# Quantized down projection: subtracting from the rows in two VectorE steps, normalisation placed behind the next tile's steps

## The chip, the core and the metric

The kernel runs on one core of a Trainium2 chip. The core has TensorE (matrix products, PE in the profile), VectorE (DVE), ScalarE (ACT), GpSimd (POOL) and SyncE (SP, here the issuer of most transfers), each with its own queue of instructions that it works through in order, and semaphores between them. The metric is the device time of one execution in microseconds; the figure shown is the median of several runs. One further execution is profiled, and its trace is what the text reads.

## What is computed

Two transformer layers on rows `x` of 2 batches x 512 rows x 512 columns, with a normalisation after every half layer. The change lies in the second half of layer 0, a feed-forward with ternary weights and truncation to 8-bit integers, and in what follows it, the attention of layer 1:

```python
x = layernorm(x + L0_attn(x))          # linear attention with a memory
# L0_ffn, quantized
xf = x / 128.0
gate = einsum("bsh,ih->bsi", xf, w_gate)
up = einsum("bsh,ih->bsi", xf, w_up)
inter = silu(gate) * up
inter_q = trunc(clip(inter * 128.0, -128.0, 127.0)).astype(int8)
down = einsum("bsi,hi->bsh", inter_q.astype(float32), w_down)
out = trunc(clip(down * 128.0, -128.0, 127.0)).astype(int8)
x = layernorm(x + out)
x = layernorm(x + L1_attn(x))          # softmax attention, one head of 128
x = layernorm(x + L1_ffn(x))           # silu(x Wg) * (x Wu), then Wd
```

`layernorm` takes the mean from each row of 512 and divides by the root of the variance plus 1e-5. The inner width of both feed-forwards is 1376, cut into 11 blocks (ten of 128 and one of 96).

## The kernel before

**Rows and order.** The 1024 rows are eight tiles of 128 rows x 512 columns, `xs[b][t]`, numbered i = 0 to 7 by `order`: tiles 0 to 3 are batch 0, tiles 4 to 7 batch 1. They stay on the core from layer to layer and are changed in place.

**Who sets the order.** All engines but GpSimd get their order of instructions from a scheduler, which starts from the order of the program and may put an instruction ahead of another that is not ready by its reckoning. GpSimd's order is that of the program as written (line 59). `tc.issue_after(ins)` keeps what is issued under it, on the engine of `ins`, behind `ins`. Each engine then follows its list strictly.

**Up half of the feed-forward (`up(b, c)`, lines 515 to 553).** For a batch and one of the 11 blocks TensorE makes gate (`pg`) and up (`pu`) in 16 matmuls, ScalarE takes the Silu (`sg`), VectorE the product (`y`, line 538) and cuts it to 12 leading bits (line 152), ScalarE makes two integer parts of it (lines 162 and 163), and VectorE joins them into `it` (line 545). The two parts are `ta`, an int8 of the positive part, and `tb`, an int16 of the negative part; the truncated value is `min(tb, 128) - ta` up to the sign that the scale carries.

**Down half (lines 570 to 614).** `down(b, t)` makes one tile of 128 rows in 11 matmuls into `pd`. `f0_down(i)` is one step of a hand-written pipeline over the eight tiles:

- `scaled(i)`: ScalarE scales `pd` into `yd` (line 592), VectorE cuts it (line 152);
- `added(i - 1)`: ScalarE makes `ta` and `tb` (lines 162, 163), VectorE joins them into `w` (line 600), GpSimd subtracts `w` from the rows (line 601);
- for tile i - 2, the statistics: VectorE `bn_stats` and `bn_aggr` (lines 132, 134), then GpSimd adds epsilon and takes the power -0.5 (lines 140, 141) into `rstd`;
- for tile i - 3, the normalisation of the rows on VectorE (line 146).

So a tile that goes through in one step of the loop has its normalisation three steps later. The calls (lines 646 to 655) run the up half's last blocks, three steps, the very last block `up(1, 10)`, four steps, then the transposes of batch 0 for the attention (`transposed(xs[0], "a10")`), then the rest.

**What follows.** `transposed` (lines 105 to 127) turns the four normalised tiles of a batch on TensorE (line 113), 16 transposes of 128 x 128 into four PSUM tiles, each of which needs all four row tiles; ScalarE copies two of them out (line 124) and VectorE the other two (line 126). From the copies TensorE makes queries and keys (`pqk`, line 752) and values (`pv`, line 765), then the same for batch 1 from tiles 4 to 7. Meanwhile GpSimd adds an output bias to all row tiles (line 805), ScalarE and VectorE split the first weights of the last feed-forward into parts (lines 675 to 689), and SyncE loads weights for it into the buffers that the quantized feed-forward has left. Then come the scores (line 779), and from about 308 us on the last feed-forward's products (lines 912 and 987).

Of the kernel before, what the change touches and what calls it, by code (L numbers as in the profile page):

```python
# [10 lines left out]
F32 = mybir.dt.float32  # L11
# [4 lines left out]
ALU = mybir.AluOpType  # L16
# [3 lines left out]
P = 128  # L20
B, S, HID = 2, 512, 512
# [15 lines left out]
def kernel(  # L37
# [19 lines left out]
    nc = tc.nc  # L57
# [14 lines left out]
    xs = [[], []]  # L72
# [32 lines left out]
    def transposed(rows, name, by_tile=False):  # L105

        xt = xtp.tile([P, NK, S], F32, tag="xt", name=f"xt_{name}")
        pts = {}

        def turn(k, t):  # L110
            if k not in pts:
                pts[k] = psum(f"pt_{name}_{k}")
            nc.tensor.transpose(pts[k][:, ts(t, P)], rows[t][:, ts(k, P)], ident)

        if by_tile:
            for t in range(NT):
                for k in range(NK):
                    turn(k, t)
        for k in range(NK):
            if not by_tile:  # L120
                for t in range(NT):
                    turn(k, t)
            if k % 2 == 0:
                copies.append(nc.scalar.copy(xt[:, k, :], pts[k]))  # L124
            else:
                copies.append(nc.vector.tensor_copy(xt[:, k, :], pts[k]))
        return xt

    def layernorm_stats(row, name):

        st = small.tile([P, 6], F32, tag="st", name=f"st_{name}")
        nc.vector.bn_stats(st, row)
        mv = small.tile([P, 2], F32, tag="mv", name=f"mv_{name}", bufs=8)
        nc.vector.bn_aggr(mv, st)
        return root(mv, name)

    def root(mv, name):

        rstd = small.tile([P, 1], F32, tag="rstd", name=f"rstd_{name}", bufs=8)
        nc.gpsimd.tensor_tensor(rstd, mv[:, 1:2], ln_eps, ALU.add)  # L140
        nc.gpsimd.tensor_tensor(rstd, rstd, minus_half, ALU.pow)
        return mv, rstd

    def layernorm_apply(out, row, stats):
        mv, rstd = stats
        nc.vector.tensor_scalar(
            out, row, mv[:, 0:1], rstd, ALU.subtract, ALU.mult
        )
# [5 lines left out]
    def truncated_parts(pool, y, n, name):  # L154

        a = pool.tile([P, S], I8, tag="tr_a", name=f"ta_{name}")  # L160
        b = pool.tile([P, S], I16, tag="tr_b", name=f"tb_{name}")
        nc.scalar.activation(a[:n], y, AF.Relu, bias=below_half[:n])  # L162
        nc.scalar.activation(b[:n], y, AF.Relu, bias=below_half[:n], scale=-1.0)  # L163
        return a, b
# [60 lines left out]
    def branch(flag):  # L225
        return nc.values_load(flag[0:1, 0:1], engines=[PE], min_val=0, max_val=1)
# [39 lines left out]
    def pair_tile(name):  # L266
        return wop.tile([P, 2, HID], F32, tag="wo", name=name)
# [6 lines left out]
    with tc.tile_pool(name="a0w", bufs=1) as a0w, tc.tile_pool(name="a0", bufs=2) as a0:  # L274
        wq = []
        for h in range(NH):
            if h % 2 == 0:
                two = query_tile(f"wq{h}").rearrange("p a (k d) -> p a k d", k=NK)
            w = two[:, h % 2]
# [10 lines left out]
        for h in range(NH):  # L290
# [3 lines left out]
            for j in range(2):  # L294
                w = pair_tile(f"wo{h}_{j}")
# [161 lines left out]
        order = [(b, t) for b in range(B) for t in range(NT)]  # L457
# [35 lines left out]
    fp = ctx.enter_context(tc.tile_pool(name="fp", bufs=2))  # L493
# [13 lines left out]
    with tc.tile_pool(name="f0", bufs=2) as f0:  # L507
# [7 lines left out]
        def up(b, c):  # L515
            n = CHUNKS[c][1]
            t = ts_up[c]
            pp = [psum(f"pg_f0{b}_{c}"), psum(f"pu_f0{b}_{c}")]
            with tc.If(ternary_up > 0) as way:
                for a in range(2):  # L520
                    for i in range(2 * NK):
                        nc.tensor.matmul(  # L522
                            pp[a][:n], t[:, a, i % NK, :n], x2[b][i],
                            start=(i == 0), stop=(i == 2 * NK - 1),
                        )
            with way.Else():
                for a in range(2):
                    for i in range(2 * NK):
                        nc.tensor.matmul(
                            pp[a][:n], gus[c][:, a, i % NK, :],  # L530
                            x2[b][i].bitcast(F32),
                            start=(i == 0), stop=(i == 2 * NK - 1),
                        )
            sg = fp.tile([P, S], F32, tag="sg", name=f"sg_f0{b}_{c}")
            nc.scalar.activation(sg[:n], pp[0][:n], AF.Silu, scale=silu_scale[:n])
            y = f0.tile([P, S], F32, tag="y", name=f"y_f0{b}_{c}")

            step = nc.vector.scalar_tensor_tensor(
                y[:n], sg[:n], eff_up[:n, 1:2], pp[1][:n], ALU.mult, ALU.mult
            )  # L540
            cut_to_12(y[:n])
            ta, tb = truncated_parts(f0, y[:n], n, f"f0{b}_{c}")

            it = its[b][c // 4][:, c % 4]
            nc.vector.scalar_tensor_tensor(  # L545
                it[:n], tb[:n], 128.0, ta[:n], ALU.min, ALU.subtract
            )
            inter[b].append(it)
            if to_divide:
                part = to_divide.pop(0)  # L550
                if part:
                    divided(*part)
            return step
# [16 lines left out]
        def down(b, t):  # L570
            pd = psum(f"pd_f0{b}_{t}")
            last = len(CHUNKS) - 1
            with tc.If(ternary_d > 0) as way:
                for c, (_, n) in enumerate(CHUNKS):
                    nc.tensor.matmul(  # L575
                        pd, inter[b][c][:n, ts(t, P)], td[c][:n].bitcast(F32R),
                        start=(c == 0), stop=(c == last),
                    )
            with way.Else():
                for c, (_, n) in enumerate(CHUNKS):  # L580
                    nc.tensor.matmul(
                        pd, inter[b][c][:n, ts(t, P)].bitcast(F32), wds[c][:n],
                        start=(c == 0), stop=(c == last),
                    )
            return pd


        pds, ys, parts, stats = {}, {}, {}, {}

        def scaled(i):  # L590
            y = f0.tile([P, HID], F32, tag="y", name=f"yd_{i}")
            nc.scalar.activation(y, pds[i], AF.Copy, scale=down_scale)
            cut_to_12(y)
            ys[i] = y

        def added(i):
            b, t = order[i]
            ta, tb = truncated_parts(f0, ys[i], P, f"d{i}")
            w = fp.tile([P, HID], F32, tag="sg", name=f"w_{i}")
            nc.vector.scalar_tensor_tensor(w, tb, 128.0, ta, ALU.min, ALU.subtract)  # L600
            nc.gpsimd.tensor_sub(xs[b][t], xs[b][t], w)  # L601

        def f0_down(i):
            if i < len(order):
                pds[i] = down(*order[i])
                scaled(i)
            if 0 <= i - 1 < len(order):
                added(i - 1)
            if 0 <= i - 2 < len(order):
                b, t = order[i - 2]  # L610
                stats[i - 2] = layernorm_stats(xs[b][t], f"f0_{i - 2}")
            if 0 <= i - 3 < len(order):
                b, t = order[i - 3]
                layernorm_apply(xs[b][t], xs[b][t], stats[i - 3])

        for c in range(3):
            up(0, c)
# [27 lines left out]
        nc.vector.tensor_scalar(down_scale, eff_d, -128.0, None, ALU.mult)  # L645
        up(1, 9)
        ternary_d = branch(flag_d)
        for i in range(3):
            f0_down(i)
        up(1, 10)  # L650
        for i in range(3, len(order) - 1):
            f0_down(i)
        xt_a1 = [transposed(xs[0], "a10")]
        for i in range(len(order) - 1, len(order) + 3):
            f0_down(i)

    gus = up_weights(gu1_in, "1", range(6, len(CHUNKS)))
# [442 lines left out]
```

## Time and profile before

| | |
|---|---|
| median of 3 runs | 493.01 us (492.49 to 493.38) |
| the profiled execution | 493.81 us, its span 492.0 us |
| granted TensorE clock, mean over the span | 0.991 |
| TensorE busy | 476.4 us (97%), 1877 instructions |
| VectorE busy | 350.6 us (71%), 673 instructions |
| ScalarE busy | 271.3 us (55%), 506 instructions |
| GpSimd busy | 126.6 us (26%), 163 instructions |
| GpSimd's subtraction (line 601) | 8 x 1438 ns |
| VectorE's join of the parts (line 600) | 8, median 687 ns, longest 1753 ns |

The span is the time from the first to the last instruction of the program; the execution's own time is 1.8 us longer. The profile is cut into 40 slices of 12.3 us in its timeline; the down half and the start of the attention lie at about 214 to 283 us, slices 18 to 23. A matmul group is given as busy if any of its matmuls is in flight, so a busy TensorE says that it is not waiting, not that it is at its peak. A releaser behind an arrow (`<-DVE x L146`) is the instruction whose end let a waiting one start. In the stretches the columns are the engines' busy times with the number of instructions, the granted clock, the share of the transfer engines and GB/s.

### The profile page before, as it was taken

Reading aid. Unit: us, or ns where it says so; the run is one execution under the profiler, and the core shown is the slowest. Engines: PE = TensorE matmul, PEld = TensorE weight load, DVE = VectorE, ACT = ScalarE, POOL = GpSimd, SP = SyncE. Lnnn points to the kernel's source line nnn. Section 1 sums busy time; section 2 is a strip of 40 time slices with the busy share of each in tenths; the row PEclk is TensorE's granted clock in tenths of the full one; section 3 lists DMA queues with packets and bytes.
Section 4 is the critical chain, followed back from the end, with each engine's and each line's share of the span. In section 5 each row is a group of like instructions: output and inputs, shape, how many; then the busy total and the mean of one; then the engine's idle time right before and its main releaser. Section 6 shows DMA issues by size and latency. Waiting matters only on the chain.

```text
span 492.0 us, 5789 instructions
## 1 busy us (share of the span) xinstructions
PE 476.4 (97%) x1877; PEld 327.3 (67%) x1877; DVE 350.6 (71%) x673; ACT 271.3 (55%) x506; POOL 126.6 (26%) x163
## 2 busy tenths in 40 slices
PE   8999999999999999999699998999999999999995
PEld 6454443444477788787556545788778888888885
DVE  1564677676775576745679988988876697999852
ACT  2344898565587585556626843556655565433220
POOL 0343102675520194003675033000000000023211
PEclk9999999999999999999989999999999999999999
DMA  8999700000060001131580000000000000000111
GB/s 286 392 339 344 277 1 1 0 0 1 2 218 15 1 1 45 46 87 33 178 308 2 0 0 1 1 2 0 0 1 0 1 1 2 0 21 23 43 45 43
DMA packets 13749, 33.99 MB, mean 69 GB/s; under 512 B 1872, under 2 KB 2768, under 8 KB 13712
## 3 DMA queue, kind: packets, MB, share of 16 engines
q1 hardware_dynamic: 13568, 33.37, 19.1%
q8 instruction: 22, 0.36, 0.3%
q14 instruction: 15, 0.12, 0.1%
q10 hardware_dynamic: 144, 0.13, 0.1%
HBM read 31.40 MB, written 2.10 MB: 68 GB/s over the span
## 4 chain that ended last, share of the span: by engine, by line
PE 68%; DVE 8%; ACT 8%; issue 3%; POOL 1%; POOLq 0%; DVEq 0%; ACTq 0%
PE pm L912 16%; PE pdm L987 8%; PE pu_f L522 8%; PE pg_f L522 8%; PE pc L912 8%; PE pdc L987 4%; PE pd_f L575 4%; DVE x L388 4%; PE pqk L752 3%; ACT y L379 2%; ACT t L398 2%; PE pv L765 1%; PE pot L820 1%; PE psc L779 1%; PE po L366 1%
## 5 line engine op out<-in xcount | busy, mean ns | idle before, releaser
L366 PE MATMUL po<-mw,q 128*128 128x512 f32 x128 | 56.8, 597 | 1.1 <-DVE x L388 0.9
L322 PE MATMUL pq<-xt_a,wq 128*128 128x512 f32 x128 | 56.5, 593 | 0.3 <-ACT xt_a L124 0.3
L366 PEld LDWEIGHTS po<-mw,q 128*128 128x128 f32 x128 | 23.2, 189 | 33.2 <-issue 18.7
L322 PEld LDWEIGHTS pq<-xt_a,wq 128*128 128x128 f32 x128 | 24.0, 190 | 29.6 <-issue 27.8
L140 POOL TENSOR_TENSOR rstd_f<-mv_f,ln_eps 128x1 f32<-128x1 f32 x16 | 3.9, 243 | 138.8 <-DVE mv_f L998 137.6
L912 PE MATMUL pm<-r,it_early 128*128 128x512 f32 x144 | 37.9, 394 | 0.9 <-ACT r L694 0.9
L912 PE MATMUL pm<-r,ugu 128*128 128x512 f32 (+1 forms) x144 | 36.8, 393 | 0.0
L912 PEld LDWEIGHTS pm<-r,it_early 128*128 128x128 f32 x144 | 26.9, 188 | 7.2 <-ACT r L694 1.3
L388 DVE SCALAR_TENSOR_TENSOR x<-po,den,x 128x511 f32<-128x511 f32 x40 | 29.8, 746 | 2.0
L912 PEld LDWEIGHTS pm<-r,ugu 128*128 128x128 f32 (+1 forms) x144 | 26.8, 186 | 6.3
L162 ACT ACTIVATE ta_f<-y_f,below_half 128x512 int8<-128x512 f32 (+1 forms) x22 | 15.9, 722 | 25.7 <-DVE y_f L152 25.4
L923 DVE SCALAR_TENSOR_TENSOR ev_q<-pm,ev_q 128x512 f32<-128x512 f32 (+1 forms) x28 | 19.2, 688 | 14.0 <-PE pm L912 14.0
L383 POOL TENSOR_TENSOR y<-y,y 128x511 f32<-128x511 f32 x16 | 20.3, 1271 | 32.1 <-ACT y L379 31.3
L400 POOL TENSOR_SCALAR td<-wd,inv_down 128x512 fp32r<-128x512 f32 (+1 forms) x11 | 19.5, 1789 | 30.3 <-DVE inv_down L196 30.3
L545 DVE SCALAR_TENSOR_TENSOR it_f<-tb_f,ta_f 128x512 fp32r<-128x512 int16 (+1 forms) x22 | 15.2, 689 | 15.4 <-ACT tb_f L163 15.3
L912 PE MATMUL pc<-r,ugu 128*128 128x512 f32 (+1 forms) x96 | 26.0, 393 | 0.0
L522 PE MATMUL pg_f<-xh,tu 128*128 128x512 f32 (+1 forms) x88 | 25.6, 406 | 0.1
L327 ACT ACTIVATE e<-pq,bq 128x512 f32<-128x512 f32 x16 | 11.1, 692 | 25.9 <-PE pq L322 25.9
L522 PE MATMUL pg_f<-xl,tu 128*128 128x512 f32 (+1 forms) x88 | 24.4, 395 | 0.1
L522 PE MATMUL pu_f<-xh,tu 128*128 128x512 f32 (+1 forms) x88 | 24.0, 394 | 0.0
L522 PE MATMUL pu_f<-xl,tu 128*128 128x512 f32 (+1 forms) x88 | 23.9, 393 | 0.0
L601 POOL TENSOR_TENSOR x<-x,w 128x512 f32<-128x512 f32 x8 | 11.5, 1438 | 44.7 <-DVE w L600 44.7
(283 smaller groups left out, 1123.7 us busy)
## 6 DMA issues: line engine op xcount, KB each, us to landing
gu<-in_gu SPq DMA_DIRECT2D x20, 512.0 KB, 8.1
wo<-in_wo SPq DMA_DIRECT2D x16, 512.0 KB, 7.4
wd<-in_wd SPq DMA_DIRECT2D x20, 256.0 KB, 5.6
x<-in_x SPq DMA_DIRECT2D x8, 256.0 KB, 4.8
wq<-in_wq SPq DMA_DIRECT2D x8, 256.0 KB, 4.4
out<-x SPq DMA_DIRECT2D x7, 256.0 KB, 2.0
gu<-in_gu SPq DMA_DIRECT2D x2, 384.0 KB, 6.5
wqkv<-in_wqkv SPq DMA_DIRECT2D x1, 768.0 KB, 10.8
```

The source lines that it names most:

```text
L162: nc.scalar.activation(a[:n], y, AF.Relu, bias=below_half[:n])
L322: nc.tensor.matmul(pq, wq[h][:, k, :], xt[:, k, :], start=(k == 0), stop=(k == NK - 1))
L366: nc.tensor.matmul(po, qs[b][h0 + j][:, ts(t, P)], mw[:, h0 + j, :], start=True, stop=True,)
L383: nc.gpsimd.tensor_add(ys[0][:, :LAST], ys[0][:, :LAST], y[:, :LAST])
L388: steps.append(nc.vector.scalar_tensor_tensor(x[:, :LAST], four[j][:, :LAST], d, x[:, :LAST], ALU.mult, ALU.add))
L400: eng.tensor_scalar(out, w, factor, None, ALU.mult)
L522: nc.tensor.matmul(pp[a][:n], t[:, a, i % NK, :n], x2[b][i], start=(i == 0), stop=(i == 2 * NK - 1),)
L545: nc.vector.scalar_tensor_tensor(it[:n], tb[:n], 128.0, ta[:n], ALU.min, ALU.subtract)
L575: nc.tensor.matmul(pd, inter[b][c][:n, ts(t, P)], td[c][:n].bitcast(F32R), start=(c == 0), stop=(c == last),)
L912: nc.tensor.matmul(p[:n], w, x, start=(left[id(p)] == begun[id(p)]), stop=(left[id(p)] == 1))
L923: nc.vector.scalar_tensor_tensor(ev[:n], pm, MAIN, ev[:n], ALU.mult, ALU.add)
L987: nc.tensor.matmul(p[:, :w], got[j // 4][1][kind][:n, j % 4], down_parts[j][kind][:, cols], start=(j == 0 and kind == kinds[0]), stop=(j = ...
```

## The change

The subtraction leaves GpSimd. `min(tb, 128) - x` goes into the rows in place, and then `-1 * that + ta`, which is the same `x - (min(tb, 128) - ta)`; both are VectorE steps, and `w` is no longer needed. The statistics are asked for in the same step of the loop, and the normalisation one step sooner (tile i - 2), held on VectorE behind the second subtraction step of tile i - 1 at that time, named by `behind`. The pipeline is thus one step shorter, and the loop around the last up block runs two steps before it instead of three.

```diff
-        pds, ys, parts, stats = {}, {}, {}, {}
+        pds, ys, stats, behind = {}, {}, {}, {}
...
         def added(i):
             b, t = order[i]
             ta, tb = truncated_parts(f0, ys[i], P, f"d{i}")
-            w = fp.tile([P, HID], F32, tag="sg", name=f"w_{i}")
-            nc.vector.scalar_tensor_tensor(w, tb, 128.0, ta, ALU.min, ALU.subtract)
-            nc.gpsimd.tensor_sub(xs[b][t], xs[b][t], w)
+
+            x = xs[b][t]
+            nc.vector.scalar_tensor_tensor(x, tb, 128.0, x, ALU.min, ALU.subtract)
+            behind[i] = nc.vector.scalar_tensor_tensor(x, x, -1.0, ta, ALU.mult, ALU.add)
+            stats[i] = layernorm_stats(x, f"f0_{i}")
 
         def f0_down(i):
...
             if 0 <= i - 2 < len(order):
+
                 b, t = order[i - 2]
-                stats[i - 2] = layernorm_stats(xs[b][t], f"f0_{i - 2}")
-            if 0 <= i - 3 < len(order):
-                b, t = order[i - 3]
-                layernorm_apply(xs[b][t], xs[b][t], stats[i - 3])
+                with tc.issue_after(behind[min(i, len(order)) - 1].ins):
+                    layernorm_apply(xs[b][t], xs[b][t], stats[i - 2])
...
-        for i in range(3):
+        for i in range(2):
             f0_down(i)
         up(1, 10)
-        for i in range(3, len(order) - 1):
+        for i in range(2, len(order) - 1):
             f0_down(i)
         xt_a1 = [transposed(xs[0], "a10")]
-        for i in range(len(order) - 1, len(order) + 3):
+        for i in range(len(order) - 1, len(order) + 2):
             f0_down(i)
```

In the order that the scheduler makes of it, VectorE's list has 673 rows where it had 665 and GpSimd's 170 where it had 178. On TensorE the matmuls of `up(1, 10)` stand before those of down tile 2 and no longer after them; on ScalarE the Silu of that block stands before the scaling of down tile 0. Tile 3's normalisation stands on VectorE directly behind tile 4's second subtraction step; the two VectorE copies of batch 0's transposes stand around tile 5's second step, its statistics and tile 4's normalisation. SyncE's list of transfers is in the same order.

## The prediction

> **What bounds the kernel now.** I read the chain of waits in order of time first, then TensorE's instructions around its largest hole, then the work of each stretch with the granted clock, then the queues that end the hole. On the chain nearly everything is TensorE (PE). Near 240 us it leaves it:
>
> ```profile
> 226.32 10.28 PE pd_f L575 x44
> 237.04 1.65 PE pd_f L575 x7
> 240.66 1.14 DVE yd L152
> 245.13 9.88 PE pqk L752 x16
> 260.34 6.87 PE pqk L752 x16
> ```
>
> Columns are start, length, engine, tile. The same 16 passes of `pqk` take 9.88 us the first time and 6.87 us the second. TensorE's own instructions there:
>
> ```profile
> 239.44 1.04 PE L113 MATMUL pt_a<-ident,x 128*128 128x128 f32 x8
> 243.57 0.86 PE L113 MATMUL pt_a<-ident,x 128*128 128x128 f32 x4 [3.09 <-DVE x L146]
> 245.13 9.88 PE L752 MATMUL pqk<-xt_a,wqkv 128*128 128x512 f32 x16 [0.70 <-ACT xt_a L124]
> ```
>
> The last four transposes of batch 0 wait 3.09 us for row tile 3's normalisation (L146), and `pqk` 0.70 us more for a copy. The stretches (PEclk is third from the end) say why `pqk` is slow afterwards:
>
> ```profile
> 235.00:240.00 5.00, 5.00 (x28) 4.08 (x27) 2.72 (x7) 1.89 (x4) 2.08 (x3) 1.00 0.34 85
> 240.00:245.00 5.00, 1.35 (x9) 0.71 (x7) 3.36 (x7) 4.26 (x9) 4.08 (x5) 0.89 0.91 277
> 245.00:250.00 5.00, 4.87 (x6) 2.14 (x7) 4.98 (x8) 1.19 (x3) 3.03 (x5) 0.50 1.04 371
> 250.00:255.00 5.00, 5.00 (x13) 2.19 (x12) 3.60 (x7) 0.69 (x1) 3.64 (x7) 0.93 1.02 408
> ```
>
> After the hole the clock is granted by half, from about 243.9 to 250.7. So the hole costs its idle time and then some 3 us again. Why tile 3 is late, on GpSimd (POOL) and VectorE (DVE):
>
> ```profile
> 240.25 1.27 POOL L601 TENSOR_TENSOR x<-x,w 128x512 f32<-128x512 f32 x1 [3.09 <-DVE w L600]
> 241.93 0.56 POOL L141 TENSOR_TENSOR rstd_f<-rstd_f,minus_half 128x1 f32<-128x1 f32 x1
> 240.66 1.14 DVE L152 TENSOR_SCALAR yd<-yd 128x512 int32<-128x512 int32 x1 [0.49 <-ACT yd L592]
> 242.33 0.67 DVE L600 SCALAR_TENSOR_TENSOR w<-tb_d,ta_d 128x512 f32<-128x512 int16 x1
> 243.01 0.51 DVE L146 TENSOR_SCALAR x<-x,mv_f,rstd_f 128x512 f32<-128x512 f32 x1
> 254.41 5.14 POOL L805 TENSOR_TENSOR x<-x,bo 128x512 f32<-128x512 f32 x4
> 254.48 1.48 DVE L146 TENSOR_SCALAR x<-x,mv_f,rstd_f 128x512 f32<-128x512 f32 x1 [0.94 <-POOL rstd_f L141]
> ```
>
> Tile 3's statistics are done by 238.2, but its root (L140, L141) stands on GpSimd behind tile 4's subtraction, which waited 3.09 us; then the normalisation stands on VectorE behind tile 5's L600. Also, a VectorE step that overlaps a 512-wide GpSimd step is held: L152 takes 1.14 instead of 0.43, L146 1.48 instead of 0.52.
>
> **The change part by part.** *Removed:* eight GpSimd subtractions (L601), 11.5 us busy with their waits (median 1.30 each), and with them the hop to GpSimd and back between a tile's subtraction and its statistics, and the holding of VectorE until the bias additions (L805). *Added:* VectorE has two steps in place of one for each tile. Neither the pair int16 with float32 nor int8 with float32 is in the trace. Nearest rows: L600 and L545 (two integer inputs, immediate scalar) 0.69 us, L331 (two float32) 0.69; above, 0.75 (L388, PSUM and a scalar from a tile) and 1.75 when GpSimd holds it; below, 0.67 (the shortest L600). I take 0.69: same operation, immediate scalar, size and memory. One follows the other at 0.61 us when it need not wait, 0.72 when it reads the other's result. So VectorE gets 8 x 0.61 to 8 x 0.72 = 4.9 to 5.8 us more.
>
> *Moved:* the normalisation comes one tile earlier in the program, held behind the next tile's second step. The last up-projection block `up(1, 10)` now precedes down tile 2. Its matmuls go from 222.46 to 219.88, down tile 2 from 219.88 to 223.58; TensorE's sum to 226.15 is equal, 0 as long as nothing waits: the block's product is read by down tile 4 alone, in its last three matmuls near 230.7, and is ready at 229.6. The block's load of the next layer (`gu` 10, SyncE's queue) can start about 2.6 us sooner; it is used past 270. But on ScalarE the block's Silu now stands in front of tile 0's scaling: it waits for `pg_f` (219.88 + 1.85), so tile 0 is scaled at 222.55 instead of 218.16. Four microseconds later, and behind it queue the cuts of every tile on VectorE.
>
> I now lay the new order of each queue out with the rows' durations. ScalarE after tile 0: `ta`, `tb` of tile 0 to 225.1; VectorE first step 225.13, the block's product 225.74, second step 226.40, the block's cut 227.01; ScalarE the block's two truncations 227.51 and 228.14, tile 1's first 228.76, tile 2's scaling 229.39 to 230.06. From the cut of tile 2 at 230.09 VectorE is full. Up to tile 3's normalisation its queue holds 5 cuts, 4 first and 4 second steps (tiles 1 to 4), 3 normalisations, 3 statistics, 3 aggregations. Start to start: 5 x 0.34 + 8 x 0.61 + 3 x 0.44 + 3 x 0.60 + 3 x 0.10 = 10.0, plus 0.5 for five places that wait 0.1 for an own or a ScalarE result. So tile 3's normalisation starts at 230.09 + 10.5 = 240.6 (before 243.01). Its root is ready by 240.6 too: the wait tied to tile 4 costs nothing here, because the root (0.09 + 0.27 + 0.55 + 0.04 after the aggregation, at 239.7) ends with it. Queued behind the tied instruction are tile 4's statistics and two copies of transposes, which TensorE wants.
>
> TensorE: transposes of tile 3 at 240.63 + 0.52 + 0.06 = 241.2 (243.57); ScalarE's first copy 241.57, free at once, `pqk` at 242.2 (245.13): **2.95 us earlier**. Its VectorE copies end at 243.1 and 245.3 and are wanted at 243.9 and 245.6, so they hide, with 0.3 us to spare; if that cover goes, TensorE waits by as much as they are late. Idle in the hole: 240.3 to 241.2 and 241.6 to 242.2, 1.5 us instead of 3.8.
>
> *The clock.* The halved stretch is 6.83 us long. Of the stretches of that length that line up with it, these are the one that ended as the clock was halved, and the least busy other one of the middle of the run, after which it stayed full (TensorE's busy time is the second figure):
>
> ```profile
> 237.05:243.88 6.83, 3.74 (x22) 2.95 (x22) 5.22 (x12) 5.04 (x8) 3.07 (x5) 1.00 0.77 213
> 291.67:298.50 6.83, 5.45 (x24) 3.25 (x24) 5.51 (x10) 3.27 (x6) 3.06 (x11) 1.00 0.00 0
> ```
>
> With 1.5 us idle such a stretch has 5.3 us or more, close to the second. So I take the clock as full: 8 x 0.859 = 6.87 us of `pqk` to 249.05 (254.85), `pv` 3.57 to 252.62 (258.43): **5.8 us earlier**, 2.85 of it from the clock.
>
> [...]
>
> *Given back:* the second transposes need tile 7. Its aggregation ends near 251.2, its root 252.1, and the bias additions start on GpSimd right behind the root (252.0), as they do in the trace, where the normalisation beside them took 1.48. It ends at 253.7, and the last transposes, wanted at 252.9, wait 0.85 us. Second `pqk` at 255.22 instead of 260.17: **-4.95 us**. Past it VectorE is full to 271 before and after, shifted as a whole, and the chain is TensorE's to 292; I carry the shift to the end.
>
> The profiled execution took 493.81 us (span 492.0, 1.8 around it), so 488.9; against the median of the runs, 493.01, it is 488.1. A part of that 0.8 may be where the halved stretch falls, which the new kernel would not have. I say **488.4**.
>
> **The rivals.** *The clock is halved all the same* (stretch at the same place). All of its 6.83 us would now meet TensorE work, 3.41 us lost; tile 7 then hides, 0.85 back. 242.2 + 6.87 + 3.57 + 3.41 = 256.0, second `pqk` 258.0: -2.15, 490.9. [...] Chance 0.17.
>
> *The gain ends at the next full engine.* VectorE is busy 4.82 and 5.00 of 5 us from 260 to 270, and GpSimd's eight bias additions now start earlier against it; if VectorE's splits were held 5 us more there, the scores would come as late as before: 493. Against: `pqk` and `pv` run without idle there, and VectorE's next result is wanted at 271. Chance 0.08.
>
> *Slower: the new steps are dear on VectorE.* The place is tile 3's normalisation, with eight of them ahead of it in a full queue. Each 0.1 us on a step is 0.8 us there; the 2.4 us of lead are gone from 0.99 us a step, and the hole with its half clock is back. At 1.3 us (twice a 512 step, or held as L600 once was) tile 3 is at 240.6 + 8 x 0.61 = 245.5, 2.5 late, and tile 7, with 14 steps ahead, at 252.1 + 8.5 = 260.6 against 258.8 when it was wanted: some 3 us slower, 496. Against: no two-input step of this form without GpSimd beside it is over 0.75. Chance 0.07.
>
> **How the numbers follow.** Forecast 0.68, clock rival 0.17, no gain 0.08, slower 0.07. The forecast's own spread: at 0.75 a step 0.9 us less gain (489.3), at 0.67 0.3 us more (488.1), runs of before 0.9 apart. 486.9 to 491.2 holds the forecast and the clock rival, without the other two. 0.2% is 1 us, about what can be told from no change: faster 0.85, same 0.07, slower 0.08.
>
> **What would show it.** Right: no 512-wide GpSimd step before the bias additions; new VectorE steps at 0.69; tile 0's scaling 4 us later; tile 3's normalisation near 240.6; first `pqk` 6.9 us long and PEclk 1.0 at 245 to 250; last transposes held by L146 of tile 7 for about 1 us. Wrong: a half clock around the first `pqk`, steps over 0.8 us, or TensorE waiting for L126 copies inside `pqk`.

## The result, and the profile of the changed kernel

| | before | changed |
|---|---|---|
| median of the first runs, 6 each | 493.13 us | 491.38 us (490.66 to 492.04) |
| ratio to before | | 0.9967, 95% interval 0.9954 to 0.998 |
| the same again, on another occasion | 493.53 us | 491.31 us; 0.9958, 0.9944 to 0.9972 |
| the profiled execution, its span | 493.81, 492.0 us | 492.04, 490.3 us |
| GpSimd, VectorE busy | 126.6, 350.6 us | 121.8, 352.2 us |
| GpSimd, VectorE instructions in the profile | 163, 673 | 155, 681 |

The change makes the kernel faster by 0.3 to 0.4%, 1.75 us in the first comparison and 2.2 in the second. The forecast was 488.4 us, and 491.38 lies just above the range. The direction was right, the size was not: more than half of the gain is missing. From line 613 on, a line of the changed kernel has a number one higher than in the kernel before (`pqk` is L753, the bias additions are L806). One run of e10 (580.88 us) and one of e11 (805.42 us) were taken at mean granted clocks of 0.781 and 0.559 and are left out of their medians and ratios below.

The TensorE instructions around the hole, in order of time (start, length):

```profile
238.90 1.04 PE L113 MATMUL pt_a<-ident,x 128*128 128x128 f32 x8
242.29 0.66 PE L113 MATMUL pt_a<-ident,x 128*128 128x128 f32 x4 [2.35 <-DVE x L146]
243.30 8.66 PE L753 MATMUL pqk<-xt_a,wqkv 128*128 128x512 f32 x16 [0.35 <-ACT xt_a L124]
257.21 7.03 PE L753 MATMUL pqk<-xt_a,wqkv 128*128 128x512 f32 x16
277.37 3.70 PE L821 MATMUL pot<-xt_p,v 128*128 128x512 f32 x8 [0.93 <-ACT xt_p L124]
```

The hole is 2.35 us where I had 0.9, the first `pqk` is still slow, and there is a new wait of 0.93 us behind the scores. The stretches show the clock (PEclk, third from the end):

```profile
235.00:240.00 5.00, 4.94 (x28) 3.92 (x26) 4.29 (x10) 4.29 (x7) 2.03 (x2) 1.00 0.41 132
240.00:245.00 5.00, 2.36 (x6) 1.26 (x7) 4.56 (x11) 2.49 (x5) 1.90 (x4) 0.80 1.02 365
245.00:250.00 5.00, 5.00 (x11) 2.19 (x10) 4.45 (x10) 1.92 (x3) 1.96 (x2) 0.86 1.04 373
```

It is granted by half again, for 3.41 us (242.98 to 246.40) and no longer for 6.83. Before, the chain of waits from the last down tile to `pqk` ran through ScalarE and VectorE and had no step of GpSimd in it; GpSimd's subtraction only lengthened VectorE's cut beside it (1.14 us). Now the chain runs through GpSimd's root steps, for which I had counted no wait (start, length, what):

```profile
235.86 0.33 DVE yd L152
236.36 1.49 POOL rstd_f L140
237.92 0.56 POOL rstd_f L141
238.51 0.55 DVE x L146
239.05 0.60 DVE st_f L132
239.66 0.59 DVE x L601
240.42 0.29 POOL rstd_f L140
240.77 0.89 POOL rstd_f L141
241.69 0.56 DVE x L146
```

These are the two root steps of a tile on 128 x 1 elements. Here is what stands beside the 1.48 us one, first VectorE, then GpSimd:

```profile
236.19 0.66 DVE L601 SCALAR_TENSOR_TENSOR x<-tb_d,x 128x512 f32<-128x512 int16 x1
236.77 0.43 DVE L152 TENSOR_SCALAR yd<-yd 128x512 int32<-128x512 int32 x1
237.10 0.69 DVE L602 SCALAR_TENSOR_TENSOR x<-x,ta_d 128x512 f32<-128x512 f32 x1
238.51 0.55 DVE L146 TENSOR_SCALAR x<-x,mv_f,rstd_f 128x512 f32<-128x512 f32 x1 [0.71 <-POOL rstd_f L141]
...
236.36 1.48 POOL L140 TENSOR_TENSOR rstd_f<-mv_f,ln_eps 128x1 f32<-128x1 f32 x1 [1.68 <-DVE mv_f L134]
```

L140 begins as L601 runs and ends at 237.84, as L602 ends; for tiles 0, 4 and 7 of the same trace it takes 0.19. VectorE then idles 0.71 us for it.

**One ruler for all traces.** The down half's first matmul starts at 214.0 to 215.4 us in the traces, on the whole later where the clock first becomes full later (at 4.05 us in the first trace of the changed kernel, whose down half starts at 214.20, and at 7.28 in e4, 215.44). So I measure from that matmul on. In us (spans are given to 0.1, so the last column is good to 0.1):

| | tile 3's normalisation | first `pqk` | second `pqk` | end of the span |
|---|---|---|---|---|
| before | 28.26 | 30.38 | 45.42 | 277.25 |
| as predicted | 25.88 | 27.45 | 40.47 | 272.30 |
| changed, first trace | 27.49 | 29.10 | 43.01 | 276.10 |
| changed, second trace (e5) | 26.68 | 28.29 | 42.38 | 275.44 |
| e8, clock full | 26.68 | 28.28 | 41.59 | 274.67 |
| e6, bias additions later | 26.67 | 28.28 | 40.64 | 273.93 |
| e10, later in two lots, clock full | 26.68 | 28.28 | 40.65 | 272.48 |
| e7, as e6, no root on GpSimd | 25.74 | 27.40 | 39.68 | 273.02 |
| e13, as e10, no root on GpSimd | 25.74 | 27.40 | 39.68 | 271.57 |
| e9, before with fillers, clock full | 28.27 | 29.84 | 43.04 | 275.81 |

### The profile page after: what moved, and what is told of

The parts are those of the page before. It is cut to its first block, busy times and chain, and to the rows that moved or that the text cites. A ratio compares the mean times of both kernels' runs of the same rounds, so it can differ in the third digit from the quotient of the medians.

```text
span 490.3 us, 5786 instructions
## 1 busy us (share of the span) xinstructions
PE 474.7 (97%) x1877; PEld 326.4 (67%) x1877; DVE 352.2 (72%) x681; ACT 271.4 (55%) x506; POOL 121.8 (25%) x155
## 4 chain that ended last, share of the span: by engine, by line
PE 61%; DVE 11%; ACT 9%; DMA 9%; issue 4%; POOL 4%; SPq 1%; POOLq 0%; DVEq 0%; ACTq 0%
PE pm L913 16%; PE pdm L988 8%; PE pg_f L522 8%; PE pc L913 8%; PE pu_f L522 8%; PE pdc L988 4%; DVE x L388 4%; DMA wo<-in_wo 3%; ACT y L379 2%; DMA wq<-in_wq 2%; DMA wqkv<-in_wqkv 2%; PE pqk L753 2%; DMA gu<-in_gu 2%; ACT t L398 2%; POOL wo L345 2%
## 5 line engine op out<-in xcount | busy, mean ns | idle before, releaser
L140 POOL TENSOR_TENSOR rstd_f<-mv_f,ln_eps 128x1 f32<-128x1 f32 x16 | 6.5, 408 | 190.0 <-DVE mv_f L999 136.1
L545 DVE SCALAR_TENSOR_TENSOR it_f<-tb_f,ta_f 128x512 fp32r<-128x512 int16 (+1 forms) x22 | 15.2, 689 | 15.1 <-ACT tb_f L163 15.0
L923 ACT ACTIVATE ev_q<-pc 128x512 f32<-128x512 f32 (+1 forms) x28 | 16.3, 591 | 10.3 <-PE pc L913 10.3
```

What stands on the lines that cost most here:

```text
L545: nc.vector.scalar_tensor_tensor(it[:n], tb[:n], 128.0, ta[:n], ALU.min, ALU.subtract)
L923: nc.scalar.activation(ev[:n], pc, AF.Copy, scale=CROSS)
```

## The experiments

The theory after the two traces had three parts: (1) GpSimd's root steps are held by VectorE's two new steps, and the normalisation waits; (2) the clock is still halved; (3) the eight bias additions, now in one row from 254.1 to 265.5 us, hold VectorE's splits, and the gain stops there. The rival to all of them was that VectorE's queue is simply longer than I had summed it.

**e1: the root off GpSimd.** The root of the down half becomes one VectorE step, without the power.

```diff
...
+        if own:
+            nc.vector.tensor_scalar(rstd, mv[:, 1:2], LN_EPS, 1e30, ALU.add, ALU.min)
+            return mv, rstd
...
```

> The changed kernel with the down half's roots taken off GpSimd: one VectorE step adds epsilon (and a minimum that changes nothing); the power -0.5 is left out in this half layer, so its rows are scaled wrongly and the time alone counts. Theory (the two tiny root steps on GpSimd are held while VectorE runs its new two-input steps back to back, and VectorE's normalisation then waits for them): no normalisation L146 of the down half waits for GpSimd any more, tile 3's starts at 240.2 to 240.9 us instead of 241.7, the first pqk 0.8 to 1.5 us sooner than 243.3; time 489.0 to 490.5 (changed kernel 491.4). Rival (VectorE's queue itself is longer than my sum of durations, the waits for GpSimd only fill time that would be lost anyway): tile 3's normalisation stays within 0.3 us of 241.7 and the time within 0.4 us of 491.4.

493.15 us, ratio 0.9987 (0.9974 to 1.0): a miss, slower than the changed kernel. The trace says why (VectorE, then GpSimd):

```profile
237.78 1.51 DVE L149 TENSOR_SCALAR x<-x,mv_f,rstd_f 128x512 f32<-128x512 f32 x1
240.50 1.39 DVE L155 TENSOR_SCALAR yd<-yd 128x512 int32<-128x512 int32 x1
241.88 1.69 DVE L605 SCALAR_TENSOR_TENSOR x<-x,ta_d 128x512 f32<-128x512 f32 x1
...
237.14 1.87 POOL L809 TENSOR_TENSOR x<-x,bo 128x512 f32<-128x512 f32 x1 [47.06 <-PE pt_a L113]
240.14 2.87 POOL L809 TENSOR_TENSOR x<-x,bo 128x512 f32<-128x512 f32 x2 [1.13 <-PE pt_a L113]
```

With nothing ahead of them in GpSimd's queue, the bias additions (here L809) begin at 237 us, in the middle of the down half, and hold VectorE there: the three steps shown take 0.54, 0.41 and 0.68 us for earlier tiles of the same trace. The roots had been the gate that kept them back. The test was confounded; e7 and e13 repeat it with the additions held by other means.

**e2: one root step instead of two.** Epsilon is added on VectorE; GpSimd keeps the power.

> The changed kernel, all of the computation kept: epsilon is added on VectorE and one GpSimd step is left in the root of the down half, the power. Theory (held root steps): the step that took 1.48 us in tile 3's root is gone, one held step of 0.9 to 1.1 us stays; tile 3's normalisation 0.4 to 1.0 us sooner than 241.7, time 490.0 to 491.0. Rival (VectorE's own queue): no more than 0.2 us sooner, 491.4, or later, as VectorE has eight more small steps (8 x 0.06 us).

492.63 us, ratio 0.9974 (0.996 to 0.9988), no better than the changed kernel. Tile 3's normalisation comes at 27.33 us on the ruler, against 26.68 in the second trace of the changed kernel. The power now starts as the second VectorE step starts and ends behind it (0.93 to 1.26 us long), and the normalisations of tiles 1 to 4 wait 0.44 each. One step is held as well as two.

**e3: twelve fillers in the hole**, matmuls of ones whose results nobody reads.

```diff
...
+            with tc.issue_after(done.ins):
+                for _ in range(fill):
+                    done = nc.tensor.matmul(idle[:, :P], ones, ones, start=True, stop=True)
...
```

> The changed kernel with 12 matmuls of ones by ones, 128 x 128 (results unused), on TensorE in the hole ahead of tile 3's transposes. Theory (the clock is halved from 242.98 to 246.40 because TensorE had little to do in the stretch ahead of it): granted clock 1.0 from 240 to 250, the first pqk 6.9 us instead of 8.66, the second pqk 1.4 to 1.8 us sooner; time 489.6 to 490.4. Rival (the clock is halved for another reason, or the filler only pushes the transposes back): the first pqk stays over 8 us and the time at 491.4 or above.

492.74 us, ratio 0.9981 (0.9969 to 0.9993). Half of it came true: the clock stays full and the first `pqk` takes 7.13 us. But eleven fillers take 2.62 us, and tile 3's transposes wait for them until 243.88, 2.6 us after their rows are ready. Too many, and in the way.

**e4: no bias additions** (the bias is left out).

> The changed kernel without GpSimd's eight additions of the output bias to the rows (that bias is left out of the result). Theory (the eight additions, now in one row from 254.1 to 265.5 us, hold VectorE's splits of the last feed-forward's weights, which lengthens 676 and 690 by 0.9 and 1.1 us and delays the first reduction of the softmax): tile 7's normalisation takes 0.52 us instead of 1.49, the split steps 676 and 690 take 2.0 and 1.3 us or less, the scores' transposes no longer wait 0.9 us at 276.4; time 1.0 to 2.5 us under the changed kernel's, 489 to 490.4. Rival (the lost 1.1 us has nothing to do with the additions): time within 0.4 us of 491.4.

489.93 us, ratio 0.9925 (0.9901 to 0.9949): 1.4 us under the changed kernel's first median. Tile 7's normalisation takes 0.55, the splits are at their short lengths, and no copy is waited for. The hole was shorter too (1.53 us), which no bias addition explains: tile 2's first root step took 0.54 here and not 1.48.

**e5: the changed kernel again.**

> The changed kernel itself again, for its ratio beside the next three and for a second trace of it. Expected: ratio to the kernel before 0.995 to 0.998, as first measured. [...]

491.31 us, ratio 0.9958. Tile 2's first root step, 1.48 us in the first trace, is 0.55, and tile 3's normalisation is at 26.68 us, as in five other traces; the first trace was the unlucky one, by 0.8 us. The clock is halved for 3.41 us all the same. Over both occasions there are twelve runs: four with a mean granted clock of 0.995 or less took 491.89 us on average, eight with 0.996 to 0.998 took 491.08. A halving of 3.41 us lowers the mean by 0.0035, so by this measure it happens in about a third of the runs (one at 0.996 could be either) and costs some 0.8 us when it does.

**e6: the bias additions later.** A small GpSimd step that reads the first softmax maximum stands ahead of them.

```diff
+    first_max = small.tile([P, 1], F32, tag="off", name="first_max")
+    nc.gpsimd.tensor_tensor(first_max, got[0][1], ln_eps, ALU.add)
     for b in range(B):
         for t in range(NT):
             nc.gpsimd.tensor_add(xs[b][t], xs[b][t], bo)
```

> The changed kernel with GpSimd's eight additions of the output bias held until the first softmax maximum is there (one small GpSimd step that reads it stands ahead of them), so they run beside VectorE's reductions, which read PSUM. All of the computation kept. Theory (the additions beside VectorE's weight splits cost the lost 1.1 us, and tile 7's normalisation 0.9 us more): tile 7's normalisation 0.55 instead of 1.49 us, splits 676, 689 and 690 at 0.75, 1.28 and 1.28 us for two, the scores' transposes wait for no copy; 0.8 to 2 us under the changed kernel of the same chip, if the additions cost nothing at their new place. Rival (the additions cost as much wherever they stand): time within 0.4 us of the changed kernel's.

490.78 us, ratio 0.9944 (0.993 to 0.9959), 0.5 us under e5 on the same chip. All three lengths came out as expected, and the second `pqk` is at 40.64. But the additions still run until 279.3 us and lengthen the next splits (0.43 to 1.50, 0.68 to 1.16); TensorE waits 1.15 us at 281.3. The cost was moved and for the most part paid again.

**e7: as e6, and no root on GpSimd** (power left out).

> The run before it with the down half's roots off GpSimd too (the power -0.5 left out, as in the first experiment), so that neither root nor addition runs on GpSimd while the down half is worked. Theory (root steps held by VectorE's two-input steps): from the first matmul of the down half to tile 3's normalisation 25.7 to 26.2 us, instead of 27.49 in the first trace of the changed kernel, with no wait for GpSimd, no normalisation over 0.6 us; 0.5 to 1.5 us under the run before it. Rival (VectorE's queue is longer than I summed): 26.5 us or more, time as the run before it.

489.46 us, ratio 0.9922 (0.9909 to 0.9936), 1.3 us under e6. Tile 3's normalisation is at 25.74 us; predicted were 25.88. So VectorE's queue was summed rightly, and the rival falls: the missing 0.9 us are the held root steps.

**e8: four fillers.**

> The changed kernel with four matmuls of ones by ones (128 x 128, about 0.24 us each, results unused) behind the last down tile's matmuls, in place of the twelve that stood in the way. Theory (the clock halves when a window of 3.41 us holds too little TensorE work): clock 1.0 from 240 to 250 us in the trace, no run with a mean clock under 0.996, transposes not later than in the changed kernel, time 0.3 to 1.5 us under it, less if most of its runs aren't halved. Rival: halved all the same, or no change.

491.31 us, ratio 0.9958 (0.9943 to 0.9972), as e5. No run has a mean clock under 0.997, and the trace is 0.8 us shorter than that of e5 on the ruler, but the median doesn't show it. By their mean clocks four of e5's six runs were not halved either, so the median has little to gain. With the clock full, TensorE is early enough to wait 0.80 us for tile 7's normalisation, for which I had 0.85.

**e9: seven fillers in the kernel before.**

> The kernel before with seven matmuls of ones by ones (128 x 128, some 1.7 us together, results unused) on TensorE between the last down tile and tile 3's transposes; nothing else changed. Theory (the clock halves when a window holds too little TensorE work, and in the kernel before this cost 2.9 us up to the second pqk, apart from the hole itself): clock 1.0 from 240 to 252 us, first pqk 7.0 us instead of 9.88, second pqk 2.7 to 3.0 us nearer to the start of the down half than 45.42 us, with tile 3's normalisation where it was. At the end 1.5 to 3 us less, since VectorE's splits beside GpSimd's additions hold part of it back: ratio 0.994 to 0.997. Rival (the clock was a consequence without a price, VectorE sets the rest): ratio over 0.998.

492.37 us, ratio 0.9978 (0.9963 to 0.9993), between the range of the theory and that of the rival. In the trace the clock is full and the second `pqk` comes 2.38 us sooner, not 2.7, since `pqk` then waits 0.65 us for a VectorE copy. Of that, 1.44 reach the end. By the mean clocks (0.996 and more in four of eleven runs) the halving was avoided only in a third of the runs.

**e10: the bias additions in two lots**, five behind the first maximum, three behind the reciprocals of the sums, with the four fillers.

> The changed kernel with the four fillers, and GpSimd's bias additions in two lots: five behind the first softmax maximum, three behind the reciprocals of the sums, so that few stand beside VectorE's splits at 274 to 281 us. All of the computation kept. Theory: second pqk as in the run with later additions (40.6 us from the start of the down half), splits behind the softmax as short as without additions, the 1.15 us wait ahead of L840 gone; ratio 0.990 to 0.993, the best of the complete kernels. Rival (the three late additions hold the roots of the attention's rows and give it back): ratio 0.9935 or above.

489.28 us, ratio 0.9906 (0.9889 to 0.9923): the best of the kernels that leave nothing out, 2 us under the changed one. TensorE no longer waits ahead of the output projection, and the 4.77 us gained at the second `pqk` all reach the end (277.25 - 272.48 = 4.77). VectorE's groups from 252 to 272 us (busy, mean ns), changed kernel and e10:

```profile
L689 DVE SCALAR_TENSOR_TENSOR it_early<-m_gu,big_gu 128x512 fp32r<-128x512 f32 x4 | 4.7, 1220 | 0.0
L676 DVE TENSOR_SCALAR m_gu<-gu 128x512 int32<-128x512 int32 x4 | 3.7, 967 | 0.0
L690 DVE TENSOR_TENSOR it_early<-it_early,m_gu 128x512 fp32r<-128x512 f32 x4 | 3.6, 951 | 0.0
L782 DVE TENSOR_REDUCE mx<-psc 128x1 f32<-128x512 f32 x2 | 1.4, 682 | 0.0
```

```profile
L786 DVE TENSOR_REDUCE mx<-psc 128x1 f32<-128x512 f32 x6 | 4.2, 692 | 0.6 <-PE psc L784 0.6
L693 DVE SCALAR_TENSOR_TENSOR it_early<-m_gu,big_gu 128x512 fp32r<-128x512 f32 x4 | 2.6, 686 | 0.0
L694 DVE TENSOR_TENSOR it_early<-it_early,m_gu 128x512 fp32r<-128x512 f32 x4 | 2.6, 686 | 0.0
L680 DVE TENSOR_SCALAR m_gu<-gu 128x512 int32<-128x512 int32 x4 | 1.5, 421 | 0.0
```

The splits take 12.0 us beside the additions and 6.7 without. In e10 the first reduction waits for TensorE (0.6); in the changed kernel it is VectorE that is late.

**e11: the two steps alone**, with the old pipeline.

> One part of the change alone: the two VectorE steps in place of VectorE and GpSimd, with the old pipeline (statistics two steps, normalisation three steps behind, up(1, 10) behind three steps). Theory (the gain of the change is tile 3's earlier normalisation, which needs the shorter pipeline too; with the old one VectorE has tile 5's cut and steps ahead of it, some 2 us): the hole 3 to 5 us, clock halved, ratio 0.997 to 1.003. Rival (the steps alone bring the gain): ratio 0.9945 to 0.997.

498.55 us, ratio 1.0095 (1.0077 to 1.0113): slower, which neither side expected. The hole is at another place:

```profile
236.11 4.27 PE L575 MATMUL pd_f<-td,it_f 96*128 96x512 f32 x9 [4.66 <-DVE it_f L545]
```

The down tiles wait 4.66 us for the product of the last up block. With `up(1, 10)` behind three tiles, its product, its cut and its join (L545, at 235.28) stand on VectorE behind steps of those tiles, the join last behind a normalisation that waits 0.93 us for a root. TensorE has no work from 231.45 to 236.11, and the clock is halved at 235.1.

**e12: the order alone**, with the subtraction on GpSimd.

> The other part alone: the shorter pipeline and the tied normalisation of the changed kernel, with the subtraction still on GpSimd behind one VectorE step. Theory: each tile's statistics wait for GpSimd's 1.3 us step right behind its VectorE step, VectorE idles or is held for over 1 us a tile, tile 3's normalisation comes later than in the kernel before: ratio 1.000 to 1.010. Rival (the order alone brings the gain): ratio 0.9945 to 0.997.

494.15 us, ratio 1.001 (1.000 to 1.002). I expected tile 3 later; it is normalised at 26.46 us, 1.8 sooner than before. It is given back further on: the normalisations of tiles 2 to 7, which now run beside the next tile's subtraction or the additions, take 1.48 to 1.52 us each, and the second transposes wait 1.35 us. Neither half of the change brings its gain alone.

**e13: both causes away.** No root on GpSimd (power left out), additions in two lots, no fillers.

> The changed kernel with no GpSimd work in the down half (root on VectorE, the power -0.5 left out) and the bias additions in two lots as in the run with fillers; no fillers. Theory (held roots and the additions beside the splits are the whole of the shortfall): the queue as I summed it for the prediction, tile 3's normalisation 25.7 to 25.9 us from the start of the down half, second pqk 39.6 to 40.5, the end 4.5 to 5.7 us nearer to the start of the down half than in the kernel before; ratio 0.988 to 0.991, which is the forecast's 488.4 against 493.0. Rival (something else is missing too): ratio 0.992 or above.

488.17 us, ratio 0.9902 (0.9887 to 0.9917). On the ruler 25.74, 39.68 and an end 5.68 us nearer. The forecast had an end 4.95 us nearer and counted 0.85 for tile 7, which this run does not pay; that the time meets the forecast so closely is in part luck. The hole is close to what I had drawn (0.9 and 0.6 us idle, here 0.60 and 0.41):

```profile
241.06 0.66 PE L113 MATMUL pt_a<-ident,x 128*128 128x128 f32 x4 [0.60 <-DVE x L149]
242.13 7.13 PE L756 MATMUL pqk<-xt_a,wqkv 128*128 128x512 f32 x16 [0.41 <-ACT xt_a L124]
```

**e14: the additions in two lots in the kernel before.**

> The kernel before with its bias additions in the same two lots; nothing else changed. Theory (in the kernel before the additions are covered: VectorE's reductions wait for the scores all the same, 0.17 us, and tile 7's normalisation is not waited for): ratio 0.998 to 1.001. Rival (the additions cost the kernel before as much as the changed one, so their place explains nothing of the shortfall): ratio 0.994 to 0.997.

493.40 us, ratio 1.0002 (0.9993 to 1.0012). In the kernel before, the additions cost nothing where they are; in the changed one, 2 us. It is the change that uncovers them, or any other gain ahead of them: e9, the kernel before with the clock full, loses 0.9 us between the second `pqk` and the end.

## Why the prediction was right in direction and wrong in size

*What bounds the kernel:* right. Tile 3's normalisation set the hole, and bringing it forward is where the gain comes from. e12 shows that this alone is not enough: 1.8 us there were lost again further on.

*The two steps:* right. They take 0.66 to 0.69 us (0.69 predicted), and no 512-wide GpSimd step is left before the bias additions.

*What is moved:* right where it was worked out. Tile 0 is scaled 7.84 us after the down half's start (222.04 - 214.20), 4.4 us later than before (218.16 - 214.75 = 3.41). But I priced the earlier `up(1, 10)` at 0 and saw only its cost on ScalarE. e11 shows what it is worth: left where it was, the new steps delay its product by 4.66 us.

*VectorE's queue to tile 3:* right as a sum (25.88 predicted, 25.74 in e7 and e13), wrong in the changed kernel (26.68, once 27.49). **The first step that failed** is "Its root is ready by 240.6 too: the wait tied to tile 4 costs nothing here". I took L140 and L141 at 0.27 (0.19 and the 0.08 up to the next step) and 0.55 us, which they take for tile 7 in the trace of the kernel before and in the first of the changed one. I had read from the profile that a GpSimd step holds VectorE's, and used it for 512-wide steps only; the same hold works the other way, on a step of one element per lane: in e5 L140, begun 0.17 us into L601, ends 0.06 us behind it. The kernel before had it too, where I could have read it: L140 of tile 3 took 0.37 us there and that of tile 5 0.64, beside VectorE's L152 and L600. Tile by tile L140 takes 0.19 to 1.48 and L141 0.55 to 1.08 in the first trace of the changed kernel. Without the root steps (e6 to e7) tile 3 is 0.93 us earlier and the second `pqk` 0.96. That run removes the steps and not only their holding, but the rows of e5 tell the two apart: VectorE idles 0.44 us for tile 1's root and 0.45 for tile 3's; at the undisturbed lengths tile 1's would have been ready before VectorE was free and tile 3's 0.1 us behind it. So nearly all of the loss is holding. The tied normalisation waits for the root itself, so the tie is not what binds; a kernel without the tie was not tried. The hold goes both ways: L140 took 0.55 us beside L601 in e5 and 0.19 for tiles 0, 4 and 7; VectorE's L605 took 1.69 beside an addition in e1 and 0.68 to 0.69 ahead of the additions. Which step began first does not settle which is held: in the first trace L140 had begun 0.41 us before L152 and 0.74 before L602, and ended behind both.

*The clock:* half right. "So I take the clock as full" holds for about two thirds of the runs and for neither trace of the changed kernel; where it fails it costs 0.8 us at the end. I also read the price of the halving, 2.85 us, from one trace of 6.83 us; in e14, with the same down half, it lasts 3.41 and the first `pqk` takes 8.66 us. And I compared stretches of 6.83 us, while the clock's changes lie on a grid of 3.41 (below).

*Given back at tile 7:* right, 0.80 us in e8 for 0.85. It too belongs to the bias additions: without them beside it the second `pqk` is 0.94 us earlier (41.59 to 40.65).

*To the end:* **the second step that failed**, "Past it VectorE is full to 271 before and after, shifted as a whole ... I carry the shift to the end". VectorE's splits can't be shifted as a whole, for the additions come earlier against them: four stood at 254 to 260 us and four behind 260 before, and now all eight run without a pause from 254.13. The splits, shown under e10 for the changed kernel, took 10.1 us before:

```profile
L688 DVE SCALAR_TENSOR_TENSOR it_early<-m_gu,big_gu 128x512 fp32r<-128x512 f32 x4 | 4.7, 1219 | 0.0
L675 DVE TENSOR_SCALAR m_gu<-gu 128x512 int32<-128x512 int32 x4 | 2.8, 748 | 0.0
L689 DVE TENSOR_TENSOR it_early<-it_early,m_gu 128x512 fp32r<-128x512 f32 x4 | 2.6, 678 | 0.0
```

Now they take 12.0. They begin 2.4 us sooner on the ruler and end only 0.4 sooner (269.64, 270.63 before, on the traces' own clocks), and the reductions that TensorE's results had paced start behind them. The chain of waits, on TensorE there before, now goes from VectorE to ScalarE and back to TensorE late (three of its pieces):

```profile
268.51 1.20 DVE it_early L690 x2
270.51 0.61 DVE mx L782
276.84 0.48 ACT xt_p L124
```

Between the second `pqk` and the end 1.2 to 1.3 us are lost in the changed kernel's traces and in e8, 0.9 in e9, nothing in e10. This is my rival "the gain ends at the next full engine", with a chance of 0.08: the mechanism was there, and its size was a loss of 1.25 us, not of all. "Against" it I had put that nothing is wanted from VectorE until 271; with TensorE 2.4 us earlier on the ruler it was wanted at 268.7 (the scores at 267.65 and the 1.07 us that lay between scores and first reduction before) and came at 270.43.

*The sum.* With all causes away 5.68 us reach the end (e13). From there the root steps take 0.91 (to e10), tile 7 0.94 and the splits 1.25, which leaves the 277.25 - 274.67 = 2.58 of e8. These terms are differences of neighbouring traces and add up by construction; what confirms them is that the roots cost 0.91 at the end from e7 to e6 too. The halved clock takes 0.8 more where it occurs (e5: 1.81). In the forecast tile 7's 0.85 was counted already; missing were the roots and the splits, some 2.2 us, and the clock in a third of the runs. What stays open is the 0.4 us between the two comparisons of the same kernel, about what the runs scatter.

## What to carry to other kernels

When work is moved from GpSimd to VectorE, cost what is left on GpSimd again: its smallest steps now stand against denser VectorE work, and here a step of 0.19 us on the chain took 0.54 to 0.55 and once 1.48 beside a VectorE instruction of 0.66. Follow a gain past the point where it is won to the next stretch in which an engine is full, and ask what starts earlier there; here GpSimd's additions, free before, cost 2 us and were freed again by holding them for a stretch in which VectorE reads PSUM (its reductions stay at 0.69 us beside them; e10, 0.9906). Before an experiment empties a queue, ask what its entries had been keeping back.

## What the runs showed of the hardware

**The clock's grid.** The clock's changes lie on a grid of 3.41 us that differs from run to run: it becomes full at 4.95 us and is halved at 243.88 in the trace of the kernel before, at 4.05 and 242.98 in the first of the changed one, and at 4.98 and 243.92 in e5, each time 70 times 3.413 us later. The busy time of TensorE (second figure) in the 3.41 us right before a halving in e5, and in a stretch on the grid of e4 that was not followed by one:

```profile
240.50:243.91 3.41, 1.62 (x7) 0.91 (x7) 2.96 (x7) 2.32 (x5) 1.38 (x3) 1.00 0.92 336
```

```profile
239.38:242.79 3.41, 1.88 (x13) 1.41 (x13) 2.96 (x8) 3.10 (x6) 1.16 (x2) 1.00 0.85 303
```

In the other traces, the last microseconds of the program left aside, halvings follow 0.00, 0.32, 0.66, 1.03, 1.50 and 1.52 us, and none follows 2.04 or more; so in these traces the bound lies between 1.62 and 1.88 us of work in 3.41. A stretch that was almost half busy was followed by a halving, and so a hole of 1.54 us can be enough (e5), though holes of 1.53 and 1.54 us in e4 and e6 were not followed by one. Transposes are counted in these figures. Counted, they separate all these cases; left out, e5's stretch has 0.96 us of work and was halved, and e4's some 0.9 and was not. In the kernel before the stretch on the grid from 4.95 to 8.36 us has 3.06 us of work, 2.34 of it transposes and some 0.9 other matmuls, and was not followed by a halving. That speaks for counting them here, at least in part.

**Who comes first.** With VectorE's order unchanged, the same 128 x 1 step on GpSimd took 1.48 us in one trace and 0.54 or 0.55 in five others (e3, e4, e5, e6, e8), and moved tile 3 by 0.8 us. It starts 0.16 to 0.17 us into a VectorE step of 0.66 in all of them. In the five it ends 0.04 to 0.06 us behind that step; in the one it is also passed by two VectorE steps that begin after it. In e11 two of these steps took 1.53 and 1.60 us, passed by later VectorE steps in the same way. What decides which engine goes on first was not found.
